# A two-layer graph kernel: the row-maximum reduce of a mixed tile and its order behind the other bank's reader

## The chip, the cores and the metric

The kernel runs on one core of one Trainium2 chip. The metric is the device time of one launch in microseconds (us); lower is better. Three runs of the kernel before gave 14,195.89, 14,200.57 and 14,211.25 us, median 14,200.57. Engines are called by their names in the profile: PE is TensorE (matmuls), PEld its weight loads, DVE is VectorE, ACT is ScalarE, POOL is GpSimd, SP issues DMAs.

## What is computed

Two layers on a graph of N = 3327 nodes with 128 features. `adj` is sparse (about 0.12% of the entries, and the diagonal).

```python
# layer 0
x = layernorm(x + rownorm(adj) @ x @ W_in + rownorm(adj.T) @ x @ W_out)
# layer 1: 128 "heads" of 8 components each
q = (x @ Wq.T).reshape(d, n, h)          # d = 128, h = 8; k, v alike
a = einsum('dnh,dmh->dnm', q, k) * d**-0.5
a = softmax(a + adj + adj, axis=2)
out = einsum('dnm,dmh->dnh', a, v).reshape(n, h * d) @ Wo.T
x = layernorm(x + out)
```

So layer 1 is full attention over all 3327 nodes, 128 times, with 8 components in a product.

## The kernel before

**Stages.** Layer 0 comes first (lines 117 to 238), then the projections to q, k and v (240 to 313), then the attention's main loop (318 to 685), then the output projection and the last layernorm. The main loop runs from about 900 to 13,840 us of the span, and everything the change touches is in it.

**Blocks and slots.** The 128 heads are taken in 32 groups of 4 (`GH`). In a group, the queries are taken in 7 blocks: six of 512 and one of 255. For one block the loop of line 649 runs over 26 tiles `t` of 128 keys, and for each tile over the four heads, two at a time (line 652): one pass of this inner loop is called a slot here. A block of 512 has 52 slots, the last block (with two heads to a bank) 26, so all in all there are 10,816. In each slot:

- PE multiplies two banks of scores `e_ps` (line 659). The two matmuls are interleaved with those of `m` (line 478, below), which use other rows of the array.
- ACT takes the exponential of each bank into `es` (line 669).
- PE multiplies the exponentials of a tile two tiles back with the values, into `o` (`products`, line 627). For most tiles these are four products of 256 columns in each of the tile's two slots. For `t = 0` and `t = 25` they are 512 wide and all come in one of the two slots, and the other one has none.

**The maxima.** The exponentials need each query's maximum over all keys, as the constant that the softmax subtracts. It is computed on its own, 38 tiles (`LEAD`, 76 slots) ahead, by a second product of q and k with queries on the partitions: one item of this stream in every slot (`next_item`). An item is a tile `m` of two PSUM banks, 128 x 1024, which PE writes with two matmuls (four for `tails`) and VectorE reduces to maxima in `mx`. For 128 queries (a row block `i`) `items_of` (line 391) yields 13 items:

- 8 of kind `all`: both banks hold scores, and one reduce of 1024 columns (line 498) takes them.
- 2 of kind `size` and 2 of kind `sums`, one pair for each of the two heads in `MIXED`. For these heads 1024 keys are stored as half sums and half differences of pairs, since the larger one of two scores is half their sum plus the absolute value of half their difference. The first bank of the `size` item holds the differences' scores, and ScalarE writes their absolute value to the tile `size` in SBUF (line 488). The first bank of the `sums` item holds the sums' scores, and VectorE adds `size` to them and takes the maximum in one instruction (line 492, out `larger`). The second bank of both holds plain scores, which VectorE reduces as a half tile of 512 columns (line 498). So a `size` tile has two readers: ScalarE for the first bank, VectorE for the second.
- 1 of kind `tails`, with the last 255 keys of all four heads.

The order of a pair is `size`, `sums`, then `all` four times, twice over, and `tails` at the end.

**Order and buffers.** From line 604 on every engine's order is the order of the program's text (`manual_schedule`); semaphores are derived from the tiles that instructions share. `max_item` is a generator that the slot's code advances, so that its instructions come between those of the slot: the matmuls of a bank of `m` ahead of each `e_ps` matmul, ScalarE's `size` between the slot's two exponentials, and the reduce after them. `m` has two buffers and `e_ps` three (lines 324, 325), so an `m` tile is written again two slots later and an `e_ps` bank by the third matmul after. `size` and `larger` have two buffers each (pool `work`).

**After the maxima.** When a block's items are done, `lowest` (line 437) takes the negated maximum over `mx` into `nm`, GpSimd splits it in two bfloat16 parts, eight slots later `to_queries` (line 451) turns it with a VectorE transpose (line 454), and six DMAs on SP's queue take it to DRAM and back into two rows of `q_st`, which the scores' matmuls of that block read.

**Beside this** GpSimd works on the graph's edges (`neighbours`), one step in every eighth slot, with gathers, products, and a few maxima on VectorE (lines 568 to 573) and an exponential on ScalarE (line 579) for each of 26 node tiles.

Of the kernel before, what the change touches and what calls it, by code (L numbers as in the profile page):

```python
# [13 lines left out]
AF = mybir.ActivationFunctionType  # L14
ALU = mybir.AluOpType
AX = mybir.AxisListType
# [12 lines left out]
NB = 512  # L29
# [36 lines left out]
def gnn_layers(ctx: ExitStack, tc: tile.TileContext, x, adj, adjt, w_in, w_out, wq, wk, wv, wo, out):  # L66


    nc = tc.nc
# [49 lines left out]
    with ExitStack() as c0:  # L119
# [9 lines left out]
        with ExitStack() as c1:  # L129
# [58 lines left out]
            for t0 in range(0, NT, 2):  # L188
# [7 lines left out]
                    op=ALU.is_equal,  # L196
# [121 lines left out]
    with ExitStack() as c1:  # L318
# [148 lines left out]
        sizes = []  # L467

        def max_item(item):

            k, q, i, *banks, kind, dst = item
            m = ps_m.tile([P, MW], F32, name="m")
            tail = N - 3 * MW
            for n, bank in enumerate(banks):
                width = NB if len(bank) == 1 else tail
                for x, (j, c0) in enumerate(bank):
                    at = n * NB + x * NB // 2
                    nc.tensor.matmul(  # L478
                        m[:, at : at + width],
                        q[64 : 64 + KR, j, i * P : (i + 1) * P],  # L480
                        k[64 : 64 + KR, j, c0 : c0 + width],
                        start=True,
                        stop=True,
                    )
                yield
            if kind == "size":
                sizes.append(work.tile([P, NB], F32, name="size"))
                nc.scalar.activation(sizes[-1], m[:, :NB], AF.Abs)  # L488
            yield
            if kind == "sums":  # L490
                larger = work.tile([P, NB], F32, name="larger")
                nc.vector.tensor_tensor_reduce(  # L492
                    larger, sizes.pop(0), m[:, :NB], scale=1.0, scalar=LOWEST, op0=ALU.add, op1=ALU.max, accum_out=dst[0]
                )
            src = m if kind == "all" else m[:, NB:]
            if kind == "tails":
                src = m.rearrange("p (n c) -> p n c", n=GH)[:, :, :tail]
            nc.vector.tensor_reduce(dst[-1], src, axis=AX.X, op=ALU.max)  # L498
            yield

        def by_node():
# [102 lines left out]
        with tc.manual_schedule(engines={ENG.PE, ENG.Activation, ENG.DVE, ENG.Pool, ENG.SP}):  # L604

            def next_item():
                item = next(stream, None)
                return max_item(item) if item is not None else iter(())
# [35 lines left out]
            for g in range(NG):  # L644
                for b, (n0, w) in enumerate(BLOCKS):
# [3 lines left out]
                    for t in range(NT):  # L649
                        pt = P if t < NT - 1 else P - (NP - N)  # L650
                        e = []
                        for j0 in range(0, GH, 2 * per):
                            m = next_item()
                            banks = []
# [22 lines left out]
                        size = NB // 2 if 0 < t < NT - 1 else NB  # L677
# [254 lines left out]
```

## Time and profile before

| what | value |
|---|---|
| median of three runs | 14,200.57 us |
| the profiled execution's own time | 14,148.77 us |
| its span, first to last instruction | 14,147.1 us |
| busy share of the span: PE, DVE, ACT, POOL | 93%, 89%, 91%, 38% |
| mean granted PE clock | 0.968 |

A line of the table of groups reads: line, engine, operation, out<-in by the program's names with partitions x elements and type, the count; then busy time in us and the mean of one in ns; then the idle time of the engine just before these instructions, and what ended most of it. A line of the waits reads: who waited, for what, us in total, times, the longest. A line of the windows has the stretch and its length, then for each of PE, PEld, DVE, ACT and POOL (or for the chosen line's engine alone) the busy time and number of instructions, then the granted clock, the DMA share and GB/s. A line of the timeline has the start and length in us, then engine, line, operation, names and count; equal neighbours are merged, and in brackets stands the idle time before and what ended it. Instructions of one engine can overlap: the end of one lies behind the start of the next. Busy shares of PE contain modelled ends.

### The profile page before, as it was taken

Reading aid. Unit: us, or ns where it says so; the run is one execution under the profiler, and the core shown is the slowest. Engines: PE = TensorE matmul, PEld = TensorE weight load, DVE = VectorE, ACT = ScalarE, POOL = GpSimd, SP = SyncE. Lnnn points to the kernel's source line nnn. Section 1 sums busy time; section 2 is a strip of 40 time slices with the busy share of each in tenths; the row PEclk is TensorE's granted clock in tenths of the full one; section 3 lists DMA queues with packets and bytes.
Section 4 is the critical chain, followed back from the end, with each engine's and each line's share of the span. In section 5 each row is a group of like instructions: output and inputs, shape, how many; then the busy total and the mean of one; then the engine's idle time right before and its main releaser. Section 6 shows DMA issues by size and latency. Waiting matters only on the chain.

```text
span 14147.1 us, 322831 instructions
## 1 busy us (share of the span) xinstructions
PE 13187.8 (93%) x131844; PEld 3737.8 (26%) x131844; DVE 12549.8 (89%) x15861; ACT 12888.5 (91%) x24068; POOL 5395.9 (38%) x4580
## 2 busy tenths in 40 slices
PE   8659999999999999999999999999999999999994
PEld 3212222222222222222222222222222222222223
DVE  7669999998999989999999989899999898999986
ACT  7549999999999989999999999999999899999992
POOL 0410000004555545555555555555555555510002
PEclk9769999999999999999999999999999999999996
DMA  6863333333434344444334434443444443321103
GB/s 251 170 101 32 29 31 31 31 30 64 72 65 67 66 62 73 68 71 70 65 64 66 72 64 72 66 72 66 64 67 70 64 70 68 68 22 17 18 7 104
DMA packets 2712108, 929.85 MB, mean 66 GB/s; under 512 B 2434977, under 2 KB 2563104, under 8 KB 2703953
## 3 DMA queue, kind: packets, MB, share of 16 engines
q1 hardware_dynamic: 2582417, 410.89, 26.1%
q0 software_dynamic: 124176, 453.33, 11.4%
q10 hardware_dynamic: 4016, 44.88, 0.9%
q8 instruction: 1034, 16.94, 0.5%
q14 instruction: 465, 3.81, 0.1%
HBM read 786.20 MB, written 151.52 MB: 66 GB/s over the span
## 4 chain that ended last, share of the span: by engine, by line
PE 62%; DVE 19%; ACT 8%; issue 5%; DMA 3%; SPq 1%; POOL 1%; another core or an unknown queue 0%; DVEq 0%; ACTq 0%; POOLq 0%
PE o L627 28%; PE m L478 28%; DVE mx L498 13%; PE e_ps L659 5%; ACT es L669 4%; ACT size L488 3%; DVE larger L492 3%; PE acc L152 1%; SPq L359 1%; POOL more L741 1%; DMA k_st<-k_d 1%; DVE top_at L160 1%; DVE top_w L159 1%; DMA k_d<-wk_sb 0%; DMA k_st<-kk_d 0%
## 5 line engine op out<-in xcount | busy, mean ns | idle before, releaser
L669 ACT ACTIVATE es<-e_ps 128x512 f32<-128x512 f32 x21632 | 11566.9, 610 | 546.5 <-PE e_ps L659 172.8
L498 DVE TENSOR_REDUCE mx<-m 128x1 f32<-128x1024 f32 (+2 forms) x10816 | 10795.7, 1050 | 1131.0 <-ACT size L488 934.6
L478 PE MATMUL m<-k_st,q_st 48*128 48x512 bf16 (+1 forms) x23296 | 6444.1, 362 | 383.2 <-DVE mx L498 166.8
L659 PE MATMUL e_ps<-q_st,k_st 50*128 50x512 bf16 (+1 forms) x23296 | 6643.1, 367 | 154.9 <-DMA q_st<-negmax_d 97.5
L627 PE MATMUL o<-es,v 128*9 128x256 f32 (+1 forms) x83456 | 6650.7, 391 | 9.1 <-ACT o_sb L636 5.2
L478 PEld LDWEIGHTS <-q_st 48*128 48x128 bf16 x23296 | 1799.4, 93 | 4980.3 <-issue 4927.3
L447 POOL CAST two<-nm 128x16 bf16<-128x16 f32 (+1 forms) x224 | 44.1, 197 | 6433.4 <-DVE nm L441 6433.4
L627 PEld LDWEIGHTS o<-es,v 128*9 128x9 f32 x83456 | 1244.8, 88 | 4211.1 <-issue 4189.6
L659 PEld LDWEIGHTS <-k_st 50*128 50x128 bf16 (+1 forms) x23296 | 1389.6, 95 | 471.6 <-issue 317.5
L492 DVE CUSTOM_DVE_ANT_0 larger<-size,m 128x512 f32<-128x512 f32 x1664 | 1126.0, 677 | 6.6 <-PE e_ps L659 5.2
L488 ACT ACTIVATE size<-m 128x512 f32<-128x512 f32 x1664 | 984.5, 592 | 136.1 <-DMA q_st<-q_d 58.2
L553 POOL TENSOR_TENSOR prod<-qn,near_rows 128x1024 f32<-128x1024 f32 x416 | 987.3, 2373 | 59.3 <-DMA near_rows<-kn_d,near 38.6
L597 POOL TENSOR_TENSOR acc<-acc,prod 128x1024 f32<-128x1024 f32 x390 | 887.4, 2275 | 30.6
L596 POOL TENSOR_TENSOR prod<-near_rows,s 128x1024 f32<-128x1024 f32 x390 | 772.7, 1981 | 7.3 <-DMA near_rows<-vn_d,near 0.4
L555 POOL TENSOR_TENSOR half<-prod 128x512 f32<-128x512 f32 x416 | 530.2, 1275 | 32.6
L522 POOL DMA_INDIRECT near_rows<-kn_d,near x416 | 418.4, 1006 | 108.9 <-issue 54.9
L522 POOL DMA_INDIRECT near_rows<-vn_d,near x416 | 413.2, 993 | 65.6 <-issue 19.9
L152 PE MATMUL acc<-a_t,x 128*128 128x512 f32 (+1 forms) x728 | 305.0, 580 | 65.6 <-DMA a_t<-in_adj_dram 43.9
L580 POOL TENSOR_TENSOR s<-s,gain 128x2048 f32<-128x2048 f32 x26 | 93.9, 3610 | 485.5 <-ACT s L579 485.5
L557 POOL TENSOR_TENSOR quarter<-half 128x256 f32<-128x256 f32 x416 | 254.9, 613 | 32.6
L152 PEld LDWEIGHTS acc<-a_t,x 128*128 128x128 f32 x728 | 141.0, 196 | 229.1 <-issue 182.3
L575 POOL COPY acc<-top 128x128 f32<-128x128 f32 x26 | 10.8, 415 | 495.7 <-DVE top L573 495.7
(155 smaller groups left out, 3534.0 us busy)
## 6 DMA issues: line engine op xcount, KB each, us to landing
q_st<-q_d SPq DMA_DIRECT2D x2304, 32.0 KB
a_t<-in_adj_dram ACTq DMA_DIRECT2D x13, 1663.5 KB
a_t<-in_adj_dram SPq DMA_DIRECT2D x13, 1663.5 KB
a_t<-in_adjt_dram SPq DMA_DIRECT2D x13, 1663.5 KB
a_t<-in_adjt_dram ACTq DMA_DIRECT2D x13, 1663.5 KB
q_d<-wq_sb SPq DMA_DIRECT2D x26, 768.0 KB
k_d<-wk_sb SPq DMA_DIRECT2D x26, 768.0 KB
k_st<-k_d SPq DMA_DIRECT2D x32, 623.8 KB
```

The source lines that it names most:

```text
L152: nc.tensor.matmul(acc[:, b, :w], x0[:, t, :], a_t[:, n0 : n0 + w], start=t == 0, stop=t == NT - 1)
L478: nc.tensor.matmul(m[:, at : at + width], q[64 : 64 + KR, j, i * P : (i + 1) * P], k[64 : 64 + KR, j, c0 : c0 + width], start=True, stop=True,
L488: nc.scalar.activation(sizes[-1], m[:, :NB], AF.Abs)
L492: nc.vector.tensor_tensor_reduce(larger, sizes.pop(0), m[:, :NB], scale=1.0, scalar=LOWEST, op0=ALU.add, op1=ALU.max, accum_out=dst[0])
L498: nc.vector.tensor_reduce(dst[-1], src, axis=AX.X, op=ALU.max)
L522: nc.gpsimd.indirect_dma_start(rows.rearrange("p d h -> p (d h)"), None, table, bass.IndirectOffsetOnAxis(ap=near[:, t, i : i + 1], axis=0))
L553: nc.gpsimd.tensor_mul(prod, qn, kg)
L596: nc.gpsimd.tensor_mul(prod, vg, share)
L597: nc.gpsimd.tensor_add(acc[:, :, :H], acc[:, :, :H], prod)
L627: nc.tensor.matmul(o[32 * j : 32 * j + VW, c : c + w], v4[:pt, j, t, :], e[j][:pt, c : c + w], start=t == 0, stop=t == NT - 1,)
L659: nc.tensor.matmul(bank[:pt, j, :w], k[: KR + 2, j0 + y * per + j, t * P : t * P + pt], q[: KR + 2, j0 + y * per + j, :w], start=True, sto ...
L669: nc.scalar.activation(es[:pt, :, :w], bank[:pt, :, :w], AF.Exp, scale=2.0)
```

## The change

In `max_item` the handles of two instructions are kept, and for a `size` item the reduce of the second bank (line 498) is declared to have no dependence on ScalarE's activation (line 488), which reads the first bank of the same tile. No instruction of the computation is added, removed or moved. Both still depend on the matmuls that write their bank, and the next matmul into the tile on both.

```diff
             if kind == "size":
                 sizes.append(work.tile([P, NB], F32, name="size"))
-                nc.scalar.activation(sizes[-1], m[:, :NB], AF.Abs)
+                taken = nc.scalar.activation(sizes[-1], m[:, :NB], AF.Abs)
             yield
...
-            nc.vector.tensor_reduce(dst[-1], src, axis=AX.X, op=ALU.max)
+            reduced = nc.vector.tensor_reduce(dst[-1], src, axis=AX.X, op=ALU.max)
+            if kind == "size":
+                tc.declare_no_dep(reduced.ins, taken.ins, reason="they read two banks of one tile")
             yield
```

## The prediction

> **What bounds the kernel now.** I read first the page's table of groups: it says which line is waited for.
>
> ```profile
> L669 ACT ACTIVATE es<-e_ps 128x512 f32<-128x512 f32 x21632 | 11566.9, 610 | 546.5 <-PE e_ps L659 172.8
> L498 DVE TENSOR_REDUCE mx<-m 128x1 f32<-128x1024 f32 (+2 forms) x10816 | 10795.7, 1050 | 1131.0 <-ACT size L488 934.6
> ```
>
> 21,632 exponentials are two to a slot, so the main loop is 10,816 slots, with one item of maxima (one reduce at L498) each. VectorE idles 1,131.0 us ahead of its reduces, and 934.6 us of that ends with ScalarE's `size`. Next, the busy time by windows, early in the loop, before GpSimd's side work starts, for all engines and for L498 alone:
>
> ```profile
> 2200.00:3200.00 1000.00, 979.89 (x10276) 264.41 (x10272) 926.19 (x1158) 970.28 (x1863) 7.59 (x38) 1.00 0.35 30
> ```
> ```profile
> 1000.00:2000.00 1000.00, 854.80 (x859) 1.00 0.35 30
> 2000.00:3000.00 1000.00, 853.18 (x857) 1.00 0.34 28
> ```
>
> TensorE shows 98%, ScalarE 97%, VectorE 92.6%; by these three numbers VectorE is last in line. A slot takes 1000/858 = 1.166 us. But the 142.0 us that the view of waits shows in 1000 to 3000 us for the reduce behind `size` is another 7.1%: VectorE is busy or in that wait all the time. Its timeline:
>
> ```profile
> 2002.30 0.69 DVE L498 TENSOR_REDUCE mx<-m 128x1 f32<-128x512 f32 x1 [0.48 <-ACT size L488]
> 2002.91 0.68 DVE L492 CUSTOM_DVE_ANT_0 larger<-size,m 128x512 f32<-128x512 f32 x1
> 2003.51 0.08 DVE L492 DVE_READ_ACCUMULATOR2_ANT mx<- 128x1 f32 x1
> ...
> 2010.43 0.69 DVE L498 TENSOR_REDUCE mx<-m 128x1 f32<-128x512 f32 x1 [0.49 <-ACT size L488]
> ...
> 2011.64 5.21 DVE L498 TENSOR_REDUCE mx<-m 128x1 f32<-128x512 f32 x5
> 2017.33 0.69 DVE L498 TENSOR_REDUCE mx<-m 128x1 f32<-128x512 f32 x1 [0.48 <-ACT size L488]
> ```
>
> Work here overlaps the tail of what ran before, so I price it from start to start. `size`'s reduce to `larger`: 2002.30 to 2002.91, 0.605. `larger` to the second reduce of `sums`: 0.603. The row of five from 2011.64 is that second reduce and four wide ones, the last running 1.21 (1,211 ns is the wide form's mean in the groups by shape): (5.21 - 0.605 - 1.21)/3 = 1.131 for a wide one. The wait costs more than its idle 0.48: without it the reduce follows the previous wide one after 1.131 instead of 1.70, so 0.57.
>
> One row block `i` has 13 items: 2 `size`, 2 `sums`, 8 `all`, 1 `tails`. VectorE: 9 x 1.131 + 2 x 0.605 + 2 x (0.603 + 0.605) = 13.81 us. With two waits, 14.95. From 2002.30 to 2017.33 are 13 items: 15.03, of which 0.12 is the transpose of L454 (2006.38 to 2006.50). The sum holds: VectorE with its wait sets the pace, and the other two only look full.
>
> TensorE and ScalarE at their own pace are seen where VectorE is not in the way:
>
> ```profile
> 7004.01 0.39 PE L659 MATMUL e_ps<-q_st,k_st 50*128 50x512 bf16 x1
> ...
> 7005.10 0.39 PE L659 MATMUL e_ps<-q_st,k_st 50*128 50x512 bf16 x1
> ...
> 7006.18 0.39 PE L659 MATMUL e_ps<-q_st,k_st 50*128 50x512 bf16 x1
> ...
> 7007.27 0.39 PE L659 MATMUL e_ps<-q_st,k_st 50*128 50x512 bf16 x1
> ```
> ```profile
> 2009.81 0.59 ACT L488 ACTIVATE size<-m 128x512 f32<-128x512 f32 x1
> 2010.28 2.07 ACT L669 ACTIVATE es<-e_ps 128x512 f32<-128x512 f32 x4
> ```
>
> TensorE: 1.085 per slot, 14.11 per 13. ScalarE with a backlog: 2009.81 to 2010.28, then (2.07 - 0.65)/3 = 0.475 each; 26 exponentials and 2 `size` are 13.3. Without the wait the three need 13.81, 14.11 and 13.3, so TensorE is next.
>
> **The change, step by step.** It takes no work away and moves none; order in every queue stays. It removes one edge: the reduce at L498 of a `size` item behind the activation at L488. 1. *VectorE's wait.* 1,664 of them at 0.57 = 949 us is the most that can go. 2. *Does it come back one instruction later?* `larger` reads `size`. Around 2002: the wide reduce started at 2000.61 (2002.30 - 0.48 - 1.21), so the next can start at 2001.74, since both banks are written at 2001.33 (second m matmul, 2000.96 + 0.37). It hands over at 2002.35; `size` ended at 2001.68 + 0.59 = 2002.27. `larger` waits for nothing as long as VectorE is behind; when it is not, the wait costs nothing. 3. *The buffer.* An m tile is reused two slots later. Its next matmul now needs both readers; ScalarE is done at 2002.27, the reduce at 2001.74 + 0.69 = 2002.43, against 2002.99 before. Earlier by 0.56.
>
> 4. *What is late next.* TensorE at 1.085, and ScalarE behind `size`. In a `size` slot ScalarE has three instructions (1.42 us against 1.085), and e_ps has three banks: the second e_ps matmul two slots later needs the first exponential of the slot between. In the trace that exponential ends at 2003.25 and this matmul starts at 2003.30, 2.56 after its `size` slot began (2000.74); at TensorE's own pace it would start 2 x 1.085 + 0.22 = 2.39 after. So 0.17 per `size`, twice per 13: 14.11 + 0.34 = 14.45 us. VectorE's 13.81 fits below that.
>
> 5. *Per 13 items* 14.95 becomes 14.45: 0.50 x 832 rounds = 416 us. VectorE's `nm` (0.14) and transpose (0.125) per query block were paid at its pace and now fit in its slack: 0.27 x 224 blocks = 60.
>
> 6. *Block edges.* At tiles t = 25 and 0 the o matmuls come as 512 wide in one slot and none in the other, so TensorE's slots there are about 1.62, 0.55, 0.55, 1.62. Before, VectorE's backlog smoothed this: 1.166 measured against (14.95 + 0.07)/13 = 1.155 leaves 0.57 us per 52 slots. With VectorE caught up it has nothing to do in the first long slot and holds TensorE back in the short ones: its wide reduce of the second item starts at 1.62 + 0.66 (when m is written) = 2.28 and gives the buffer back at 3.54, where TensorE wants it at 2.72: 0.82. So 0.3 more, x 224 = -67.
>
> 7. *Added waits.* The matmul that reuses the m tile waits for two engines, and `larger` for ScalarE. An added semaphore instruction shows as 51 ns on TensorE's queue (L478, 480 of them now) and 21 on VectorE's (L492). 1,664 x 51 = 85 us if bare, 0 if the queue runs ahead over the 0.55 us of o matmuls; below nothing it cannot be. VectorE's 35 us lie in its slack. I take 0 and keep 85. GpSimd's phase costs VectorE some five maxima per node tile (26 tiles), up to 65 us, part of which may now hide: taken as 0. DMA: loads of q start two hops ahead and their 97.5 us of TensorE stalls stay; a pace 3% higher takes 3% off their lead.
>
> Sum: 416 + 60 - 67 = 409 us off. The profiled execution was 14,148.77 (span 14,147.1), so 13,740; the runs' median is 0.37% above it, and from 14,200.57 the same 409 gives 13,790.
>
> **Rivals.** *A, more:* steps 4 and 6 don't bite, and TensorE's 1.085 or VectorE's 13.81 binds alone. 14.95 - 14.11 = 0.84 x 832 = 699, + 60 = 759: 13,440; all 949 gone: 13,250. For it: TensorE's waits for ScalarE's exponentials are only 57 us now. Against: they are covered by VectorE's, which is what goes. *B, less:* ScalarE binds. For it, 97% busy; then the gain is what it idles for TensorE's e_ps, the 172.8 us above: 14,030. Against: its rows overlap, 0.475 start to start against 0.59 long. The Trainium skill (Perfetto Trace Analysis, Identifying the Most-Contended Engine) names the engine of highest occupancy and calls occupancy a fair measure for ScalarE, which is this rival; the trace disagrees by the 0.475. *C, nothing:* the declared pair isn't the edge that holds the reduce, or another wait holds it at the same point: 14,200. Against: the row names `size` 1,615 times, and m is written long before. *D, slower:* the added wait instructions stand bare at the head of TensorE's m matmuls and pay 85 us, with VectorE's 35 behind them, while the gain is nothing: 14,285 to 14,320. It decides if TensorE, not VectorE, already sets the pace, so that its queue has no slack. For it, 98% busy; against, 1.085 against 1.166.
>
> **How the numbers follow.** Forecast 0.62, A 0.16, B 0.09, C 0.06, D 0.07. Predicted 13,790. The range drops C, D and what of A lies beyond its 759: 13,440 to 14,080; it takes in B, and the 85 us on the forecast or on B all but 35. About 0.2% (28 us) is what a measurement of this kernel can tell from no change. Faster 0.87, same 0.06, slower 0.07.
>
> **What would show it.** Step 1: VectorE's wait for `size` falls from 934.6 to under 100 us. Step 2: `larger` shows little wait for `size`. Steps 4 and 5: about 888 items per 1000 us in the early windows instead of 858; TensorE's waits for exponentials grow from 57 us. Step 6: idle TensorE time for the reduce gathers at block edges. Step 7: more semaphore instructions at L478 and L492. If `size` is waited for as before, C holds; if TensorE never waits for ScalarE and items pass 910, A.

## The result and the profile after

The changed kernel took 13,866.67 us (median of four runs, 13,855.61 to 13,915.66) against 14,198.23 for the kernel before: ratio 0.977, interval 0.975 to 0.980, 332 us less. The forecast was 13,790, 409 less. Its profiled execution has a span of 13,868.3 us where the one before had 14,147.1; these single executions differ by 279 us only, since the one before ran 0.37% below the median of its runs.

The groups of the page after (two lines were added, so L659, L669 and L627 are now L661, L671 and L629):

```profile
L671 ACT ACTIVATE es<-e_ps 128x512 f32<-128x512 f32 x21632 | 11447.3, 610 | 368.4 <-PE e_ps L661 169.2
L498 DVE TENSOR_REDUCE mx<-m 128x1 f32<-128x1024 f32 (+2 forms) x10816 | 10656.3, 1052 | 314.8 <-PE m L478 201.3
...
L492 DVE CUSTOM_DVE_ANT_0 larger<-size,m 128x512 f32<-128x512 f32 x1664 | 1144.8, 688 | 512.9 <-PE e_ps L661 465.6
```

VectorE's idle time ahead of its reduces fell from 1,131.0 to 314.8 us, and ScalarE's `size` is gone from its causes. Half of it came up again one instruction later: 512.9 us ahead of `larger`, 465.6 of it until a matmul ends (the row names e_ps, but `larger` reads m; the two matmuls run side by side). The windows after, all engines, then L498 alone:

```profile
2200.00:3200.00 1000.00, 986.16 (x10556) 231.06 (x10548) 952.71 (x1187) 987.64 (x1915) 13.59 (x41) 1.00 0.37 33
```
```profile
1000.00:2000.00 1000.00, 863.27 (x878) 0.99 0.35 31
2000.00:3000.00 1000.00, 867.33 (x882) 1.00 0.34 29
```

There are 880 items per 1000 us instead of 858. TensorE rose only from 98.0 to 98.6% busy and ScalarE from 97.0 to 98.8%, while the pace rose by 2.6%, so TensorE's busy share had not been its distance to a bound. Here is VectorE's timeline around a `size` item, then TensorE's (e_ps, and one matmul of m), then ScalarE's:

```profile
2002.90 2.94 DVE L498 TENSOR_REDUCE mx<-m 128x1 f32<-128x1024 f32 x3
2006.03 0.69 DVE L492 CUSTOM_DVE_ANT_0 larger<-size,m 128x512 f32<-128x512 f32 x1 [0.19 <-PE e_ps L661]
2006.65 0.08 DVE L492 DVE_READ_ACCUMULATOR2_ANT mx<- 128x1 f32 x1
2006.65 5.81 DVE L498 TENSOR_REDUCE mx<-m 128x1 f32<-128x512 f32 x6
2012.68 0.69 DVE L492 CUSTOM_DVE_ANT_0 larger<-size,m 128x512 f32<-128x512 f32 x1 [0.23 <-PE e_ps L661]
```
```profile
2004.17 0.39 PE L661 MATMUL e_ps<-q_st,k_st 50*128 50x512 bf16 x1
...
2005.30 0.39 PE L661 MATMUL e_ps<-q_st,k_st 50*128 50x512 bf16 x1
2005.51 0.37 PE L478 MATMUL m<-k_st,q_st 48*128 48x512 bf16 x1
...
2006.39 0.39 PE L661 MATMUL e_ps<-q_st,k_st 50*128 50x512 bf16 x1
...
2006.73 0.37 PE L661 MATMUL e_ps<-q_st,k_st 50*128 50x512 bf16 x1
...
2007.59 0.39 PE L661 MATMUL e_ps<-q_st,k_st 50*128 50x512 bf16 x1
...
2008.67 0.39 PE L661 MATMUL e_ps<-q_st,k_st 50*128 50x512 bf16 x1
```
```profile
2005.11 0.59 ACT L488 ACTIVATE size<-m 128x512 f32<-128x512 f32 x1
2005.58 3.54 ACT L671 ACTIVATE es<-e_ps 128x512 f32<-128x512 f32 x7
```

The first row of three is a wide reduce, `tails` and the reduce of `size`, which follows with no idle time before it. VectorE then waits 0.19 ahead of `larger`. TensorE's slots start 1.09 apart (2007.59 to 2008.67: 1.08). Only the slot two after the `size` slot of 2004.17 is longer, 2006.39 to 2007.59 = 1.20 here: its second e_ps matmul starts 0.34 after the first instead of 0.22. That matmul, at 2006.73, writes the bank that the second of the seven exponentials reads, and by the trace this one ends at 2006.68, late because `size` ran ahead of it. Over all full blocks, at the seven `size` places behind the first one, this matmul starts 0.05 us behind the end of that exponential (in the median, and in the lowest and the highest tenth too).

From the traces of this kernel, of the one before and of three experiments below I worked out one more table: the median distance in us between the first e_ps matmuls of successive slots, by the slot's place in its block of 52 (counted from 0), over the 192 full blocks. A `size` item is issued at places 2, 8, 15, 21, 28, 34, 41 and 47; places 2 to 5 hold the uneven o products and are called the block's edge here. The last column adds up all 52 places, by means.

```
place              2     3     4     5  |   9    10    11    12  |  15    16    17    18  | 52 places*
before           1.514 0.791 1.229 1.774 | 1.235 1.205 1.130 1.132 | 1.128 1.176 1.207 1.130 | 61.14
after            1.513 0.567 1.538 1.707 | 1.088 1.252 1.088 1.087 | 1.087 1.088 1.254 1.088 | 59.49
no size          1.513 0.442 1.553 1.537 | 1.088 1.087 1.087 1.087 | 1.119 1.088 1.089 1.088 | 58.13
size first       1.513 0.750 1.470 1.775 | 1.544 1.087 1.087 1.087 | 1.087 1.546 1.088 1.088 | 61.61
before, more mid 1.514 0.794 1.228 1.774 | 1.175 1.206 1.131 1.131 | 1.129 1.178 1.206 1.729 | 62.97
* sum of the means of the slots under 4 us; a longer one is a stall, counted apart
```

### The profile page after: what moved, and what is told of

Same layout as the page of the kernel before. It is cut to its first block, busy times and chain, and to the rows that moved or that the text cites. A ratio compares the mean times of both kernels' runs of the same rounds, so it can differ in the third digit from the quotient of the medians.

```text
span 13868.3 us, 323334 instructions
## 1 busy us (share of the span) xinstructions
PE 12943.0 (93%) x131844; PEld 3262.7 (24%) x131844; DVE 12554.3 (91%) x15861; ACT 12768.7 (92%) x24068; POOL 5382.8 (39%) x4580
## 4 chain that ended last, share of the span: by engine, by line
PE 75%; DVE 9%; ACT 6%; issue 3%; DMA 3%; POOL 1%; SPq 1%; another core or an unknown queue 0%; DVEq 0%; ACTq 0%; POOLq 0%
PE o L629 37%; PE m L478 33%; PE e_ps L661 5%; DVE mx L498 5%; ACT es L671 4%; DVE larger L492 1%; DMA k_st<-k_d 1%; DVE top_at L160 1%; DVE top_w L159 1%; POOL more L743 1%; SPq L359 0%; ACT size L488 0%; ACT unread L150 0%; DMA negmax_d<-turned 0%; PE pr L288 0%
## 5 line engine op out<-in xcount | busy, mean ns | idle before, releaser
L671 ACT ACTIVATE es<-e_ps 128x512 f32<-128x512 f32 x21632 | 11447.3, 610 | 368.4 <-PE e_ps L661 169.2
L498 DVE TENSOR_REDUCE mx<-m 128x1 f32<-128x1024 f32 (+2 forms) x10816 | 10656.3, 1052 | 314.8 <-PE m L478 201.3
L661 PE MATMUL e_ps<-q_st,k_st 50*128 50x512 bf16 (+1 forms) x23296 | 6822.9, 367 | 275.0 <-DMA q_st<-negmax_d 144.7
L478 PE MATMUL m<-k_st,q_st 48*128 48x512 bf16 (+1 forms) x23296 | 6538.0, 368 | 212.2 <-DMA q_st<-q_d 118.0
L629 PE MATMUL o<-es,v 128*9 128x256 f32 (+1 forms) x83456 | 6651.4, 391 | 16.8 <-issue 11.4
L478 PEld LDWEIGHTS <-q_st 48*128 48x128 bf16 x23296 | 1425.3, 94 | 5098.6 <-issue 4954.3
L629 PEld LDWEIGHTS o<-es,v 128*9 128x9 f32 x83456 | 1243.8, 88 | 4386.2 <-issue 4364.7
L492 DVE CUSTOM_DVE_ANT_0 larger<-size,m 128x512 f32<-128x512 f32 x1664 | 1144.8, 688 | 512.9 <-PE e_ps L661 465.6
L661 PEld LDWEIGHTS <-k_st 50*128 50x128 bf16 (+1 forms) x23296 | 1403.2, 95 | 367.6 <-issue 193.8
```

The source lines that it names most:

```text
L478: nc.tensor.matmul(m[:, at : at + width], q[64 : 64 + KR, j, i * P : (i + 1) * P], k[64 : 64 + KR, j, c0 : c0 + width], start=True, stop=True,
L492: nc.vector.tensor_tensor_reduce(larger, sizes.pop(0), m[:, :NB], scale=1.0, scalar=LOWEST, op0=ALU.add, op1=ALU.max, accum_out=dst[0])
L498: reduced = nc.vector.tensor_reduce(dst[-1], src, axis=AX.X, op=ALU.max)
L629: nc.tensor.matmul(o[32 * j : 32 * j + VW, c : c + w], v4[:pt, j, t, :], e[j][:pt, c : c + w], start=t == 0, stop=t == NT - 1,)
L661: nc.tensor.matmul(bank[:pt, j, :w], k[: KR + 2, j0 + y * per + j, t * P : t * P + pt], q[: KR + 2, j0 + y * per + j, :w], start=True, sto ...
L671: nc.scalar.activation(es[:pt, :, :w], bank[:pt, :, :w], AF.Exp, scale=2.0)
```

## The experiments

The kernel before took 14,140 to 14,243 us (medians), depending on the chip. So each kernel is compared by its ratio to the kernel before on the same chip; 0.01 of it is 142 us. The changed kernel is 0.977.

**Half of the declaration.**

```diff
-            if kind == "size":
+            if kind == "size" and banks[0][0][0] == 0:
                 tc.declare_no_dep(reduced.ins, taken.ins, reason="they read two banks of one tile")
```

> The changed kernel with the declaration kept for the first of the two mixed heads only, so that in each row block of 13 items one of the two reduces still waits for ScalarE. Theory (each stretch of six or seven items is paced by itself, because m has only two buffers: VectorE with its wait in one, TensorE plus ScalarE's backlog in the other): about half of the 332 us is lost again, 14,032 us (13,990 to 14,070). Rival, the averages decide: VectorE needs 13.81 + 0.57 = 14.38 us per 13 items, still under TensorE's 14.45, so the wait that is left costs nothing: 13,870 to 13,900.

Ratio 0.991 (0.989 to 0.993): 132 us off, about 40% of the gain. The rival (0.977 to 0.979) falls. The places show it as well: by medians the seven slots 9 to 15, which hold the wait that was left, take 8.09 us, as in the kernel before (8.09; changed 7.78), and the six slots 16 to 21 take 6.64 (before 6.91, changed 6.69). So averages over 13 items don't decide: VectorE does not make up in one stretch for a wait in another. That this is for the two buffers of m between it and TensorE fits, but no run has another number of buffers.

**No `size`.** ScalarE's activation is left out, and `larger` adds zeros.

```diff
-                taken = nc.scalar.activation(sizes[-1], m[:, :NB], AF.Abs)
+                sizes.append(still)            # one tile of zeros
...
-                tc.declare_no_dep(reduced.ins, taken.ins, ...)
```

> The changed kernel without ScalarE's size (the absolute values of the half differences are left out; larger adds a tile of zeros instead), all else the same. Theory (TensorE sets the pace at 1.085 a slot and loses 0.165 us behind each of the 1,664 size instructions, since the exponentials behind it free their bank late): 275 us less than 13,867, so 13,590 (13,540 to 13,640), and the slots two after a size slot take 1.09 instead of 1.25 us. Rival, ScalarE's load sets the pace: 1,664 x 0.475 = 790 us less, 13,080. Rival, VectorE still sets it, by the wait of 466 us that the profile shows ahead of larger: 13,400.

Ratio 0.958 (0.957 to 0.960), so 271 us below the changed kernel where the theory says 275 and the rival, ScalarE's load, 790. In the table the slots of 1.25 are 1.09. So ScalarE doesn't set the pace by its load, but costs 0.165 us behind a `size` by holding a bank of e_ps. That the total fits so well is in part luck. By means, 0.37 us per block, 77 us in all, goes at the edge (places 2 to 8 sum to 8.31 instead of 8.68), where the theory has one `size` of the eight, 34 us; the other places give 206 us instead of 240, as some of them (15, 28 and 39) now take 1.12 to 1.13.

**`size` ahead of the exponentials**, on the kernel before.

```diff
+                if n == 1 and kind == "size":
+                    sizes.append(work.tile([P, NB], F32, name="size"))
+                    nc.scalar.activation(sizes[-1], m[:, :NB], AF.Abs)
                 yield
-            if kind == "size":
-                sizes.append(work.tile([P, NB], F32, name="size"))
-                nc.scalar.activation(sizes[-1], m[:, :NB], AF.Abs)
             yield
```

> The kernel before, with its dependence, but ScalarE's size issued ahead of the slot's first exponential instead of between the two. size then ends some 1.03 us into the slot, before VectorE is free at 1.08, so VectorE's wait of 935 us goes without the declaration. Theory: the first exponential of the slot ends 0.475 later, and the second e_ps matmul of the next slot waits for it: 0.27 us per size in place of 0.165, 1,664 x 0.105 = 175 us more than the changed kernel: 14,040 (13,980 to 14,100). Rival, VectorE's wait was all there is and ScalarE's order costs nothing: 13,867.

Ratio 1.008 (1.007 to 1.010): slower than before, and outside both expectations. Rows of its timeline around one `size`, from three engines:

```profile
2009.11 0.38 PE L478 MATMUL m<-k_st,q_st 48*128 48x512 bf16 x1
...
2009.52 0.60 ACT L487 ACTIVATE size<-m 128x512 f32<-128x512 f32 x1 [0.19 <-PE e_ps L659]
...
2010.02 1.08 ACT L669 ACTIVATE es<-e_ps 128x512 f32<-128x512 f32 x2
2010.15 0.69 DVE L498 TENSOR_REDUCE mx<-m 128x1 f32<-128x512 f32 x1 [0.37 <-ACT size L487]
...
2010.66 0.37 PE L659 MATMUL e_ps<-q_st,k_st 50*128 50x512 bf16 x1
```

`size` reads the first bank, but starts at 2009.52, behind the matmul of the second (2009.11 + 0.38 = 2009.49): I had it start 0.2 earlier. So the slot's first exponential ends at about 2010.61 (2010.02 + 0.59), and the second e_ps matmul of the next slot starts right behind, at 2010.66. That slot takes 1.54 us in the table: 0.46 lost per `size`, not 0.27. The mechanism is the expected one; its price was set too low. By that price the kernel would lie 1,664 x (0.46 - 0.165) = 490 us above the changed one; measured are (1.0082 - 0.9772) x 14,198 = 440. The other part of the expectation failed too: VectorE's wait for `size` did not go but is 637.3 us, against 934.6. It became shorter and the kernel slower all the same.

**One more VectorE reduce**, behind `tails`, first on the changed kernel, then on the one before.

```diff
+            if kind == "tails":
+                nc.vector.tensor_reduce(again, src[:, :2], axis=AX.X, op=ALU.max)
```

> The changed kernel with one more VectorE reduce (half of the tails tile once more, 510 columns, into a tile that nobody reads) in each 13 items. Theory: VectorE now has slack, 13.81 + 0.605 = 14.42 us per 13 items against TensorE's 14.45, so most of it hides: 13,867 to 14,010, less than a third of the work added. Rival, VectorE still sets the pace: 832 x 0.605 = 503 us more, 14,370.

> The kernel before with the same one more VectorE reduce of 510 columns in each 13 items. Theory: before the change VectorE with its wait sets the pace, so the added work shows whole: 832 x 0.605 = 503 us, 14,700 (14,640 to 14,740). Rival, VectorE's wait was slack and another engine set the pace: within 100 us of 14,198.

On the changed kernel: ratio 0.998 (0.997 to 0.999), 295 us above it, between the two expectations and twice what the theory allows. The theory's number was an average over 13 items, which the first experiment rules out. For the one stretch of seven slots that ends in `tails`, VectorE needs 0.605 + 1.208 + 4 x 1.131 + 1.127 + 0.605 = 8.07 us, TensorE 7 x 1.087 + 0.165 = 7.77: 0.30 x 832 = 250. The places say more: by medians the seven slots 9 to 15 take 8.35 us instead of 7.78, the 13 slots 9 to 21 take 14.98 instead of 14.47, and the block's edge loses next to nothing (places 2 to 8, by means: 8.73 instead of 8.68). So in the middle of a block most of the added 0.605 shows. What the sum leaves out is VectorE's idle time ahead of `larger`, 0.19 to 0.21 us in the median, twice per 13 items, in this run. With it VectorE is busy or in that wait nearly all the time, and its slack in the changed kernel is about 0.1 us per 13 items (0.605 less 0.51), not the 0.6 between 13.81 and 14.45.

On the kernel before: ratio 1.010 (1.009 to 1.012), 145 us instead of 503. It lies between the two expectations, nearer to the rival, and so speaks against the claim that VectorE set the pace of the kernel before. But the view of the reduces' line says how long they waited for `size` in this run (us, times):

```profile
  ACT size L489: 582.3, 861
```

Without the added reduce these were 934.6 us in 1,615 waits. `tails` is followed by `size`, whose reduce waits; the added 0.605 us stood in that wait of 0.57 and used it up. By places (medians), slot 15 takes 0.60 more (1.725), and the six slots 16 to 21 give 0.38 of it back (6.53 instead of 6.91). To tell this from the rival, the same work was put where no wait follows.

**One more reduce in the middle of a stretch**, on the kernel before.

```diff
-                yield plain[j][2]
+                yield (*plain[j][2][:2], "all" if n else "more", plain[j][2][3])
...
+            if kind == "more":
+                nc.vector.tensor_reduce(again, m[:, NB:], axis=AX.X, op=ALU.max)
```

> The kernel before with one more VectorE reduce of 512 columns (bank two of m once more, into a tile that nobody reads) in each 13 items, but behind the first wide item after sums instead of behind tails. Theory: behind tails the same work cost only 1.0% because the next instruction is the reduce that waits for size, and the added 0.605 us stood in that wait of 0.57; in the middle of a stretch no wait follows at once, but the stretch still ends at the next size, whose start is set by TensorE's slot, and that by the reduce two items before it, so here the added work goes into the pace whole: 832 x 0.605 = 503 us, 3.5% (2.9 to 3.7%). Rival, VectorE's own work did not set the pace of the kernel before: about 1.0% again.

Ratio 1.027 (1.025 to 1.028): 378 us, three quarters of 503 and under the expected 2.9%. The places say why: place 18 goes from 1.130 to 1.729, as do 31 and 44, so three of a block's four added reduces show whole. The fourth falls to the block's edge and costs nothing (places 2 to 5 as before). So VectorE with its wait set the pace of the kernel before everywhere but at the edges.

**The block's edge: even products for the last tile**, on the changed kernel.

```diff
-                        stop=t == NT - 1,
+                        stop=t == NT - 1 and not parts,
...
-                if t == NT - 1:
+                if t == NT - 1 and not parts:
...
-                        size = NB // 2 if 0 < t < NT - 1 else NB
+                        size = NB // 2 if t else NB
```

(The copy of o and its DMAs then take both parts at once; these lines are left out here.)

> The changed kernel with the o products of the last key tile (t = 25) split over its two slots like those of the other tiles, so that of the four uneven slots at a block's edge (1.51, 0.57, 1.54, 1.71 us) the first pair becomes two even ones; the copy of o to SBUF follows the second part. Theory: at an edge VectorE has nothing to do in the long slot and holds TensorE back in the short ones, 0.98 us per block over even slots; half of it goes, 0.5 x 192 = 96 us: 13,770 (13,730 to 13,810). Rival, the edge's loss comes from the one pair that is left, or from the copy of o: 13,850 to 13,880.

Ratio 0.978 (0.977 to 0.979): nothing gained, as the second expectation has it. The four slots became 1.087, 1.087, 1.018 and 2.135, with the same sum of 5.33: the loss moved into the pair that is left.

**The lead of the maxima**: `LEAD = 44` for 38.

> The changed kernel with the maxima 44 key tiles ahead of the exponentials instead of 38 (12 more slots). Theory: TensorE's idle time until a block's maxima have come back from DRAM into q (144.7 us in 15 waits, with 97.5 before the change) is a matter of lead; 12 slots are 13 us, the waits are up to 31 us, so more than half of it goes: 80 us less, and some 11 us more ahead of the first exponential: 13,800 (13,760 to 13,840). Rival, the transfers are late by their queue and not by lead, so the waits stay: 13,867 to 13,890.

Ratio 0.975 (0.974 to 0.976), some 33 us off: between the two expectations, and with an interval that overlaps that of the changed kernel, so not clear of noise. TensorE's waits for q did shrink; here they are (us, times, longest), in the changed kernel and then in this one:

```profile
PE e_ps L661 <- DMA q_st<-negmax_d: 144.7, 15, 30.7
```
```profile
PE e_ps L661 <- DMA q_st<-negmax_d: 40.7, 5, 23.7
```

That is 104 us less. But the sum of 52 places rose from 59.49 to 59.68 (40 us), above all at places 3 to 6, where other items now met the edge, and the first e_ps matmul came 23 us later.

**Other items at the edge**: `LEAD = 42`; **o copied by VectorE** (`nc.vector.tensor_copy` for `nc.scalar.copy`); and **both**.

> The changed kernel with the maxima 42 key tiles ahead instead of 38. It shifts which items meet a block's four uneven slots: with 38 they are size, sums, all, all; with 42 all, all, all, all (and tails behind). Theory: at an edge ScalarE's backlog holds TensorE, because size and the copy of o (0.475 each) fall into the short slots, and a wait of 0.52 for an exponential's bank is seen there; without size there the four slots fall from 5.37 to some 5.0, 0.35 x 208 = 73 us, and the waits for q become shorter by half as they did with 44, 70 us, less 8 us ahead of the first exponential: 135 us less than the changed kernel, ratio to before 0.968 (0.965 to 0.971). Rival (the prediction's own step 6): VectorE holds TensorE back there, and four wide reduces make it worse: 0.976 to 0.980.

> The changed kernel with the copy of o to SBUF, once per block, on VectorE instead of ScalarE. Theory (ScalarE's backlog at the edge): ScalarE has 0.475 less to do in the short slots, VectorE idles in the long slot before them (0.74 us ahead of larger in one edge of the trace): 0.3 us per block, 70 us, ratio to before 0.972 (0.970 to 0.975). Rival, VectorE is the one that is late at the edge: 0.977 to 0.981.

> Both of the two last together: the changed kernel with the maxima 42 tiles ahead and o copied by VectorE. Theory: with no size at the edge, ScalarE's backlog there is small either way, so the copy's move adds little to what 42 gives: ratio to before 0.966 (0.963 to 0.970). Rival, the two add up: 0.963. Rival, VectorE with four wide reduces and the copy is late: 0.972 or more.

The ratios are 0.971 (0.970 to 0.973), 0.974 (0.972 to 0.975) and 0.976 (0.974 to 0.977). The first (13,836.4 us beside 14,243.3 for the kernel before on its chip) is faster than the changed kernel too, as their intervals lie apart. But it gains some 84 us of the 135 expected, and mostly for one of the two reasons: q's waits fell to 84.5 us, while the means of places 2 to 5 sum to 5.28 instead of 5.37, not 5.0. With the copy on VectorE, place 5 fell from 1.745 to 1.551 (means), 40 us as a sum over blocks, and the ratio lies in the range of that theory, though its interval ends where that of the changed kernel begins. Together the two are worse than each, as the third expectation has it: places 2 to 5 sum to 5.46. So ScalarE is late at the edge with `size` there (a wait of 0.52 in the changed kernel's trace),

```profile
2345.73 0.37 PE L661 MATMUL e_ps<-q_st,k_st 50*128 50x512 bf16 x1 [0.52 <-ACT es L671]
```

and VectorE is late with wide items or the copy. TensorE's idle times between 0.15 and 4 us at places 2 to 6, added up by what ended them over all full blocks, bear this out. In the changed kernel they are 95 us for ScalarE's exponentials and 47 for VectorE's reduces (before the change 29 and 82); with the copy on VectorE 3 and 127; with the lead of 42 they are 35 and 65; with both 2 and 151. Without `size`, in the run further up, they are 41 and 83, and places 2 to 5 sum to 5.03. Neither engine alone accounts for the loss there, which stays at 0.8 to 1.1 us per block against even slots (4 x 1.087) in the four runs that moved work at the edge, and at 0.7 without `size`.

**The changed kernel again.**

> The changed kernel as it is, once more. It came out 332 us faster where 409 were forecast; in its trace TensorE waited 144.7 us for q's rows of maxima instead of 97.5, and slots over 4 us held 164 us instead of 112. Theory (the higher pace shortens the lead and so lengthens those waits): 135 us or more again for q, and a ratio of 0.977 (0.975 to 0.979). Rival (such waits differ from chip to chip and run to run, whatever the pace): about 100 us for q in this profile, and a ratio of 0.973 to 0.975.

Ratio 0.977 (0.975 to 0.978), and 135.0 us of waits for q: as the theory says. Over all traces with a lead of 38 these waits are 135 to 145 us for the five with a ratio below 0.98, and 92 to 117 for the six others. The two groups stay apart on each of the two chips that ran kernels of both, which speaks against the rival. But the waits don't grow step by step with the pace: 142.2 us at a ratio of 0.958 beside 144.7 at 0.977, and 110.4 at 1.027 beside 92.0 at 1.008. So a shorter lead fits, and is not the whole account.

## Why the prediction was right, point by point

- *Pace before* (14.95 us per 13 items, VectorE and its wait): right. Places 9 to 21, 22 to 34 and 35 to 47 sum to 15.00, 15.08 and 15.03 us by medians, and added VectorE work shows whole in the middle of a stretch.
- *Steps 1 and 3*, the wait: it is gone for every `size`, and TensorE's waits for VectorE's reduces ahead of m did not rise (166.8 us before, 87.9 after).
- *Step 2*: wrong in its reason. The wait does come back ahead of `larger`, 466 us, where VectorE was to wait for nothing or at no cost. The step looked at `size` (done at 2002.27) and left out the matmuls of the tile of `sums`, which `larger` reads too. In the trace before, the second of them ends at 2002.46, behind the 2002.35 at which VectorE was to be free:

```profile
2002.09 0.37 PE L478 MATMUL m<-k_st,q_st 48*128 48x512 bf16 x1
```

  So `larger` waits for TensorE and not for `size` (7.2 us), and the wait is longer than the matmul's lateness by the delay told in the last section. It hardly hurt the forecast, as the next point shows: 13 slots take the time that was forecast.
- *Steps 4 and 5*, what is late next: right to 0.03. 14.45 was forecast; the three sums of 13 places are 14.47, 14.48 and 14.48, the even slots 1.087 (so are the rows that the prediction shows: 3.26/3; it took 1.085), and the slot two after a `size` 1.252, that is 0.165 more (forecast 0.17). Leaving `size` out removes these. TensorE's waits for exponentials grew from 57.0 to 126.7 us, as forecast. But "13.81 fits below" was too easy: with its wait ahead of `larger` VectorE is close to the pace as well, as the added reduce shows. In the early windows 880 items came per 1000 us, not 888.
- *Step 6*, the edge: its size is right, its cause only in part, so the size is in part luck (its own 0.82 - 0.57 is 0.25, taken as 0.3). Places 2 to 8 sum to 8.67 before and 8.68 after by means; the forecast had the gain of seven slots (0.31) cancelled by 0.3. But in the trace the longer idle times there end with ScalarE's exponentials, 95 us, and those for VectorE's reduces fell from 82 to 47. Four tries at the edge moved the loss without removing it.
- *Step 7*, added waits: TensorE got no added instruction (480 at L478 before and after, so 0 was right). VectorE got 503 (1,161 to 1,664 at L492). The stalls for q did not stay at 97.5 us but became 144.7. This is a term that was mis-sized: slots over 4 us hold 164 us instead of 112. The second trace and the lead of 44 fit the shorter lead as its cause.
- *The sum.* 59.49 instead of 61.14 per block is 1.65 x 208 = 343 us (10,816 slots are 208 blocks of 52), where steps 5 and 6 had 1.97 x 208 = 409. Less 53 for the long slots and 20 for a first e_ps matmul that came later (1,009 instead of 989 us; it varies from 987 to 1,024 over the kernels with this lead, so the change isn't needed for it) that is 270 of the 279 us between the two spans. What of 1.97 - 1.65 is missing was not traced: by medians the block gains 1.79, so nearly half of it lies in slots that are longer only now and then. One trace also doesn't fix the size of these parts: the second trace of the changed kernel has 59.75 per block, 54 us more in all, and a span of 13,942.8 us.

The rivals: *A* fell, since the 0.165 stays. *B*, ScalarE binding by its load, fell by the result, which is more than its 172.8 us, and by the run without `size`: 271 us, not 790. By the Trainium skill (Perfetto Trace Analysis, Identifying the Most-Contended Engine) ScalarE, with a higher occupancy than VectorE, would have been the engine to relieve first; here taking a wait from VectorE, the lower one at 92.6%, gave 2.3%. *C* and *D* fell by the result.

## What to carry to other kernels

Price a wait by the distance from start to start of the work around it, and add up an engine's own work and its waits before comparing engines: the one with the lowest busy share can be the one that sets the pace. Then do the same sum for the next engines, stretch by stretch and with the waits that the change will leave them: here no engine made up in one stretch for a wait in another. When you ask whether an instruction will wait, list everything that it reads. When added work is used to test for a bound, its place decides: the very wait that is in question must not stand behind it.

## What the runs showed that was not expected

An added semaphore instruction can delay more than the 21 ns that its row shows. In the changed kernel `larger` starts at 2006.03, though the last matmul of its tile ends at 2005.88 (2005.51 + 0.37) and `size` at 2005.70 (2005.11 + 0.59): 0.15 us later. In the 1,629 waits of that trace in which the matmul ends last, the median is 0.147 us, some 240 of the 512.9 us of idle time ahead of `larger`. A reduce that waits for TensorE starts 0.038 us behind its matmul, and so does `larger` itself in the run without `size`, where it doesn't wait for ScalarE. Where `size` ends last (187 waits with the lead of 44) it is 0.032. So it isn't waiting for two engines as such that costs the 0.11, but which of the two the separate instruction waits for. By the semaphores in the trace that is TensorE here: when the matmul ends last, that instruction starts 0.042 us behind it and `larger` 0.105 later. (Ends of matmuls are modelled in the profile, in all of these alike.) What this costs the changed kernel was not tested.

And `size` and `larger`, which each read one bank of m, start only behind the matmul of the other bank, in the two traces shown: the program orders them by whole tiles there. This made `size` 0.2 us later in the run that put it first.
